# Moving more of the product with C from VectorE to GpSimd in a Mamba scan, from the second image on

## The chip, the cores and the metric

The kernel runs on one core of one Trainium2 chip. The metric is the device time of one execution in microseconds (us). Engines are called PE (TensorE, with PEld for its weight loads), DVE (VectorE), ACT (ScalarE), POOL (GpSimd) and SP (SyncE).

## The reference

Four layers act on x of shape 4 x 384 x 48 x 48; each adds its result to its input. Layer 0, a Mamba block, holds the change. Per image, its 48 x 48 pixels are a sequence of L = 2304 steps, with 768 inner channels and 16 states per channel:

```
dt = softplus(dt @ dt_proj_w.T + dt_proj_b);  A = -exp(A_log)
dA    = exp(dt_t[..., None] * A)
dBx   = dt_t[..., None] * B_t[:, None, :] * x_t[..., None]
h_new = dA * h_prev + dBx
y_t   = einsum('bds,bs->bd', h_new, C_t)
```

The rest of layer 0 is projections, a short convolution, gates, an output projection and a norm. Layer 1 is a 1x1 product, an 8x8 patch transform, a depthwise 3x3 convolution (nine taps) with a gelu gate, and a 1x1 product. Layer 2 is a depthwise 11x11 convolution. Layer 3 mixes four experts with two matrix products each.

## The kernel before

All data is float32. An image's 2304 steps are cut into five chunks of 460 to 464 steps (`CHUNKS`, `NC = 5`). In a chunk the 768 channels are six tiles of 128 partitions, taken as three pairs; a pair of tiles has 2 x 16 states, so a chunk has `LEN = 96` (tile, state) units and the kernel 20 x 96 = 1920. A unit is called u here, and one pass of the main loop is a slot. `where(u)` (L797) gives the chunk i, the pair p, the tile m, the state s and whether the unit is "slow". Within a pair, the position q runs from 0 to 31: an even q and the odd q after it are the two tiles of one state, and they share one row of B and one of C, broadcast to 128 partitions by a DMA from SP (`spread`, L802).

One unit passes through these steps:

- `decay` (L820, ACT): da = exp(dt * A), into one of two PSUM buffers.
- `drive` (L831, POOL): bu = u * B, into one of three SBUF buffers.
- `scan` (L844, DVE): the recurrence along 460 steps from da and bu. In a slow unit it is written to the SBUF buffer g, in any other unit back into da.
- `keep` (L858, ACT): the last column is copied to `carry`, for the next chunk of the same image; the last chunk of an image needs none.
- the product with C: `product_now` (L864, DVE, g = da * C) in a unit that isn't slow, `product` (L873, POOL, g = g * C in place) in a slow one.[...]
- `turned` (L770, PE): g is transposed in four pieces and added up over the states in the PSUM tile y. There are six buffers of g.

The order in each engine's queue is written out by hand in the main loop (L1067 to L1103). Slot u holds, in this order: the ACT steps of the other work, `scan(u)` (in a slow unit followed at once by its `keep`), the other engines' steps of the other work, `product_now(u)` with its `keep`, `decay(u + 2)`, `product(u - 1)` and `drive(u + 3)`. The transposes follow five slots after a slow unit and three slots after another.

The other work is generators of steps (`Task`, `Lane`). The lane `aux` holds the rest of layer 0, with due times by slot. Lane `one` holds layers 1, 2 and the router of the image before (`later`), lane `two` its experts. A `Meter` limits the PE work that the lanes put into a slot to about 2.3 us, by written-in weights. The first image runs with nothing but `aux`; lanes `one` and `two` are filled from the 42nd slot of the second image on. When the 1920 units are over, what is left of the lanes, the last image's layers 1 to 3 and its experts run in a tail, with no scans.

The depthwise taps of layer 1 (L1264 and L1266, DVE) go three to a slot when `slow_slot()` (L1116) is true, else two: a slow slot has no product on DVE. `place[0]` there is the slot that is being written.

Of the kernel before, what the change touches and what calls it, by code (L numbers as in the profile page):

```python
# [21 lines left out]
DI, DS, DTR, DCONV = 768, 16, 24, 4  # L22
# [117 lines left out]
def tile_layers(ctx: ExitStack, tc: tile.TileContext, a: dict, out: bass.AP):  # L140
# [272 lines left out]
    with ExitStack() as first:  # L413
# [123 lines left out]
        NC = len(CHUNKS)  # L537
# [18 lines left out]
        def scans(wk, mm, ring, meter, place, lanes, begin):  # L556
# [240 lines left out]
            def where(u):  # L797
                i, q = divmod(u, LEN)
                p, q = divmod(q, PAIR)
                return i, p, 2 * p + q % 2, q // 2, q % 3 == 0  # L800

            def spread(k, which):  # L802

                if not 0 <= k < N // 2:
                    return
                i, p, m, s, _ = where(2 * k)
                (b, t), c = G[i], st[i]
                n = CHUNKS[t]
                tag = "BC"[which]
                v = wk.tile([P, TM], F32, name=f"{tag}{b}_{t}_{p}_{s}", tag=tag, bufs=3 + which)  # L810
                live[tag, k] = v
                live.pop((tag, k - 3 - which), None)
                nc.sync.dma_start(v[:, :n], c["bc"][which, s, :n].partition_broadcast(P))

            def decay(u):
                i, p, m, s, _ = where(u)
                (b, t), c = G[i], st[i]
                n = CHUNKS[t]
                da = live["da", u] = mm.tile([P, 512], F32, name=f"da{b}_{t}_{m}_{s}", tag="da")
                nc.scalar.activation(  # L820
                    da[:, :n], c["dt", p][:, m % 2, :n], AF.Exp, scale=a_neg[:, m, s : s + 1]
                )

            def drive(u):
                i, p, m, s, _ = where(u)
                (b, t), c = G[i], st[i]
                n = CHUNKS[t]
                bu = live["bu", u] = wk.tile(
                    [P, TM], F32, name=f"bu{b}_{t}_{m}_{s}", tag="bu", bufs=3
                )  # L830
                nc.gpsimd.tensor_mul(  # L831
                    bu[:, :n], c["u", p][:, m % 2, :n], live["B", u // 2][:, :n]
                )
# [280 lines left out]
                ordered[0] = False  # L1114

        def slow_slot():  # L1116
            return place[0] % (2 * DS) % 3 == 0

        def later(b, ring, accr):

# [123 lines left out]
            def finish_strip(hb):  # L1244
# [7 lines left out]
                def taps(ct):  # L1252
                    yield ("dve", 0, (accr, 1))
                    acc, k = sums[ct] = accr.take(f"dw{b}_{hb}_{ct}")
                    v = acc[:, :LB].rearrange("p (h w) -> p h w", w=W)
                    room = 3 if slow_slot() else 2
                    for k in range(9):
                        if not room:
                            yield ("dve",)
                            room = 3 if slow_slot() else 2  # L1260
                        room -= 1
                        src = d["pad", hb][:, ct, k // 3 : k // 3 + 8, k % 3 : k % 3 + W]
                        if k == 0:
                            nc.vector.tensor_scalar_mul(v, src, w_dw[:, ct, 0:1])  # L1264
                        else:
                            nc.vector.scalar_tensor_tensor(  # L1266
                                v, src, w_dw[:, ct, k : k + 1], v, ALU.mult, ALU.add
                            )
# [479 lines left out]
        place = [0]  # L1748
# [187 lines left out]
```

## Time and profile before

| | us |
|---|---|
| median of 3 runs (lowest, highest) | 5467.04 (5466.89, 5471.5) |
| the profiled execution's own time | 5472.59 |
| its span | 5470.3 |
| first to last scan | 88.7 to 4551 |
| first scan of the second image | 1025.0 |

Busy shares of the span: PE 86%, DVE 76%, POOL 57%, ACT 55%. A share is an average over stages that differ: up to 1025 us the first image's scans run alone, from there to 4551 us three images' scans run beside the later layers of the images before, and after that there are no scans. A row of groups gives line, engine, operation, tiles and count, then busy time and mean ns of one, then idle time of the engine before them and what ended it.

### The profile page before, as it was taken

Reading aid. Unit: us, or ns where it says so; the run is one execution under the profiler, and the core shown is the slowest. Engines: PE = TensorE matmul, PEld = TensorE weight load, DVE = VectorE, ACT = ScalarE, POOL = GpSimd, SP = SyncE. Lnnn points to the kernel's source line nnn. Section 1 sums busy time; section 2 is a strip of 40 time slices with the busy share of each in tenths; the row PEclk is TensorE's granted clock in tenths of the full one; section 3 lists DMA queues with packets and bytes.
Section 4 is the critical chain, followed back from the end, with each engine's and each line's share of the span. In section 5 each row is a group of like instructions: output and inputs, shape, how many; then the busy total and the mean of one; then the engine's idle time right before and its main releaser. Section 6 shows DMA issues by size and latency. Waiting matters only on the chain. (4 is left out here: it accounts for less than half of the span.)

```text
span 5470.3 us, 82006 instructions
## 1 busy us (share of the span) xinstructions
PE 4689.8 (86%) x27796; PEld 3688.4 (67%) x27796; DVE 4176.4 (76%) x5806; ACT 2999.9 (55%) x6632; POOL 3124.6 (57%) x2795
## 2 busy tenths in 40 slices
PE   5677677777678989988899999988899999999899
PEld 3445445454447767665678887665678878888799
DVE  5889989999898898899988788899988774443200
ACT  3555555565458765655467655665566753334321
POOL 3878878865567777665567667665666662000000
PEclk8788888798789999999899999999999999999899
DMA  4445445454345555544566566554556564543200
GB/s 121 135 137 147 124 128 146 128 149 124 104 125 148 151 160 163 172 140 140 152 169 174 155 166 175 153 154 130 164 158 169 163 175 145 148 138 102 66 27 23
DMA packets 628393, 758.97 MB, mean 139 GB/s; under 512 B 58869, under 2 KB 622181, under 8 KB 627582
## 3 DMA queue, kind: packets, MB, share of 16 engines
q1 hardware_dynamic: 617668, 751.98, 48.5%
q8 instruction: 221, 3.62, 0.3%
q10 hardware_dynamic: 10298, 1.67, 0.2%
q14 instruction: 206, 1.69, 0.1%
HBM read 663.81 MB, written 89.65 MB: 138 GB/s over the span
## 5 line engine op out<-in xcount | busy, mean ns | idle before, releaser
L831 POOL TENSOR_TENSOR bu<-u,B 128x460 f32<-128x460 f32 (+1 forms) x1920 | 2226.4, 1168 | 1118.2 <-DVE g L844 506.7
L820 ACT ACTIVATE da<-dt,a_neg 128x460 f32<-128x460 f32 (+1 forms) x1920 | 1243.7, 649 | 317.3 <-DVE g L864 223.0
L770 PE MATMUL y<-ident,g 128*115 128x128 f32 (+1 forms) x7680 | 1169.0, 295 | 273.4 <-DVE g L864 202.0
L770 PEld LDWEIGHTS y<-ident,g 128*115 128x115 f32 (+1 forms) x7680 | 1024.1, 185 | 546.9 <-DVE g L864 246.8
L844 DVE TENSOR_TENSOR_SCAN da<-da,carry,bu 128x460 f32<-128x460 f32 (+1 forms) x1008 | 1182.5, 1173 | 69.9 <-ACT da L820 48.7
L873 POOL TENSOR_TENSOR g<-g,C 128x460 f32<-128x460 f32 (+1 forms) x660 | 767.7, 1163 | 197.9 <-ACT carry L858 195.9
L864 DVE TENSOR_TENSOR g<-da,C 128x460 f32<-128x460 f32 (+1 forms) x1260 | 796.4, 632 | 87.1 <-DMA C<-bcd 28.1
L844 DVE TENSOR_TENSOR_SCAN g<-da,carry,bu 128x460 f32<-128x460 f32 (+1 forms) x528 | 616.8, 1168 | 105.6 <-ACT da L820 61.1
L858 ACT COPY carry<-da 128x1 f32<-128x1 f32 x1008 | 159.0, 158 | 948.1 <-DVE g L864 944.8
L1601 PE MATMUL pout<-hr,we 128*128 128x144 f32 x3456 | 488.9, 298 | 49.7 <-ACT hr L1617 30.5
L1601 PEld LDWEIGHTS pout<-hr,we 128*128 128x128 f32 x3456 | 461.1, 199 | 70.2 <-ACT hr L1617 40.6
L1601 PE MATMUL ph<-xe,we 128*128 128x144 f32 x3456 | 471.1, 292 | 15.2 <-DMA xe<-x3d 10.1
L1601 PEld LDWEIGHTS ph<-xe,we 128*128 128x128 f32 x3456 | 448.6, 195 | 30.4 <-DMA xe<-x3d 8.9
L1408 PE MATMUL pc<-band,row 128*128 128x162 f32 (+14 forms) x3456 | 456.2, 285 | 7.1 <-ACT row L1395 7.1
L1408 PEld LDWEIGHTS pc<-band,row 128*128 128x128 f32 x3456 | 443.5, 195 | 11.0 <-ACT row L1395 8.3
L642 PE MATMUL pin<-xch,w_inx 128*128 128x463 f32 (+2 forms) x720 | 332.5, 602 | 33.4 <-DMA xch<-in_x 20.0
L1266 DVE SCALAR_TENSOR_TENSOR dw<-pad,w_dw,dw 128x384 f32<-128x384 f32 x576 | 347.6, 614 | 17.4 <-ACT pad L1241 6.5
L915 PE MATMUL po<-w_out,zs 128*115 128x384 f32 (+1 forms) x960 | 342.4, 497 | 9.3 <-DVE dt L750 7.8
L674 PE MATMUL pinz<-xch,w_inz 128*128 128x460 f32 (+1 forms) x720 | 326.3, 592 | 0.3 <-DVE ye L1633 0.3
L1617 ACT ACTIVATE hr<-ph,nb 128x144 f32<-128x144 f32 x576 | 176.2, 376 | 268.2 <-PE ph L1601 267.8
L844 DVE TENSOR_TENSOR_SCAN da<-da,nil,bu 128x460 f32<-128x460 f32 x252 | 294.8, 1170 | 12.8 <-ACT carry L858 8.5
L1375 ACT ACTIVATE rep<-x,br,wr 128x192 f32<-128x192 f32 x576 | 274.1, 540 | 21.0 <-DVE br L1345 20.9
(202 smaller groups left out, 5725.4 us busy)
## 6 DMA issues: line engine op xcount, KB each, us to landing
B<-bcd SPq DMA_DIRECT2D x768, 230.0 KB, 3.5
C<-bcd SPq DMA_DIRECT2D x768, 230.0 KB, 3.8
B<-bcd SPq DMA_DIRECT2D x192, 232.0 KB, 3.7
C<-bcd SPq DMA_DIRECT2D x192, 232.0 KB, 4.0
xe<-x3d SPq DMA_DIRECT2D x192, 216.0 KB, 2.9
ye<-y3d SPq DMA_DIRECT2D x144, 216.0 KB, 2.8
y3d<-ye SPq DMA_DIRECT2D x96, 216.0 KB, 2.2
xs<-x1d SPq DMA_DIRECT2D x24, 576.0 KB, 4.9
```

The costliest lines, as they stand in the source:

```text
L642: nc.tensor.matmul(ps[:, lo : halo + n], lhsT=w_inx[:, k, bass.ts(j, P)], rhs=c["x"][:, k, lo : halo + n], start=k == 0, stop=k == CT - 1,)
L674: nc.tensor.matmul(ps[:, :n], lhsT=w_inz[:, k, bass.ts(j, P)], rhs=c["x"][:, k, DCONV - 1 : DCONV - 1 + n], start=k == 0, stop=k == CT - 1,)
L770: nc.tensor.matmul(c["y", m][:w, bass.ts(k, P)], lhsT=src[:, bass.ts(k, w)], rhs=ident, is_transpose=True, start=c["terms", m] == 1 and k ...
L820: nc.scalar.activation(da[:, :n], c["dt", p][:, m % 2, :n], AF.Exp, scale=a_neg[:, m, s : s + 1])
L831: nc.gpsimd.tensor_mul(bu[:, :n], c["u", p][:, m % 2, :n], live["B", u // 2][:, :n])
L844: nc.vector.tensor_tensor_scan(here[:, :n], da[:, :n], bu[:, :n], last if t else nil[:, 0:1], ALU.mult, ALU.add,)
L864: nc.vector.tensor_mul(live["g", u][:, :n], live["h", u][:, :n], live["C", u // 2][:, :n])
L873: nc.gpsimd.tensor_mul(g[:, :n], g[:, :n], live["C", u // 2][:, :n])
L915: nc.tensor.matmul(ps[:w, :C], lhsT=c["zs"][:, m, bass.ts(k, w)], rhs=w_out0[:, m, :], start=m == 0, stop=m == MT - 1,)
L1266: nc.vector.scalar_tensor_tensor(v, src, w_dw[:, ct, k : k + 1], v, ALU.mult, ALU.add)
L1408: nc.tensor.matmul(d["acc2"][0][:, : BANDS[k] * W].rearrange("p (h w) -> p h w", w=W)[:, lo - edges[k] : hi - edges[k], xlo:xhi], lhsT=d[" ...
L1601: nc.tensor.matmul(ps[:, bass.ts(m, EB)], lhsT=w[:, k, bass.ts(m, P)], rhs=of[:, k, :], start=k == 0, stop=k == CT - 1,)
```

## The change

Before, a unit is slow when q mod 3 is 0: 11 of the 32 units of a pair of tiles. After, this holds in the first image (i < 5) only; from the second image on a unit is slow when q mod 4 is 0 or 1, which are the two tiles of every other state: 16 of 32. `slow_slot` takes the second rule for all slots.

```diff
@@ -797,7 +797,8 @@
             def where(u):
                 i, q = divmod(u, LEN)
                 p, q = divmod(q, PAIR)
-                return i, p, 2 * p + q % 2, q // 2, q % 3 == 0
+                slow = q % 3 == 0 if i < NC else q % 4 < 2
+                return i, p, 2 * p + q % 2, q // 2, slow
...
         def slow_slot():
-            return place[0] % (2 * DS) % 3 == 0
+            return place[0] % 4 < 2
```

## The prediction, made before the result was known

> **What bounds the kernel now.** I first read the groups of the page for the four operations of a unit.
>
> ```profile
> L831 POOL TENSOR_TENSOR bu<-u,B 128x460 f32<-128x460 f32 (+1 forms) x1920 | 2226.4, 1168 | 1118.2 <-DVE g L844 506.7
> ...
> L844 DVE TENSOR_TENSOR_SCAN da<-da,carry,bu 128x460 f32<-128x460 f32 (+1 forms) x1008 | 1182.5, 1173 | 69.9 <-ACT da L820 48.7
> L873 POOL TENSOR_TENSOR g<-g,C 128x460 f32<-128x460 f32 (+1 forms) x660 | 767.7, 1163 | 197.9 <-ACT carry L858 195.9
> L864 DVE TENSOR_TENSOR g<-da,C 128x460 f32<-128x460 f32 (+1 forms) x1260 | 796.4, 632 | 87.1 <-DMA C<-bcd 28.1
> ```
>
> The same product costs 632 ns on DVE and 1163 ns on POOL. POOL's drives sit idle for 1118 us, most of it until a DVE scan gives a bu buffer back: POOL follows DVE.
>
> Next I cut the time at each chunk's first scan and read the busy times of the stretches. The columns are stretch, length, and busy us (count) of PE, PEld, DVE, ACT, POOL, then the granted PE clock and DMA. The first row is the first image, the second the three images that the change touches, the third the tail; then come some of the 15 chunks.
>
> ```profile
> 89.00:1025.00 936.00, 669.39 (x2960) 455.95 (x2960) 846.93 (x1035) 536.55 (x1122) 771.98 (x686) 0.80 0.48 135
> 1025.00:4551.00 3526.00, 3107.01 (x18334) 2403.62 (x18335) 3067.40 (x4193) 2152.39 (x4742) 2344.11 (x2087) 0.93 0.54 154
> 4551.00:5470.00 919.00, 866.46 (x6354) 798.64 (x6353) 233.84 (x516) 287.90 (x736) 4.96 (x15) 0.96 0.31 88
> ```
>
> ```profile
> 1025.00:1230.00 205.00, 159.71 (x738) 106.24 (x738) 188.06 (x251) 126.44 (x277) 157.78 (x144) 0.90 0.53 146
> 1230.00:1505.00 275.00, 197.89 (x762) 122.15 (x762) 248.81 (x355) 136.48 (x295) 156.46 (x142) 0.78 0.40 114
> ...
> 2656.00:2906.00 250.00, 222.27 (x1350) 178.09 (x1349) 213.41 (x296) 152.09 (x353) 156.62 (x138) 0.92 0.57 161
> 2906.00:3143.00 237.00, 230.26 (x1603) 198.98 (x1602) 186.64 (x243) 168.64 (x397) 154.70 (x138) 0.98 0.57 162
> ...
> 3591.00:3855.00 264.00, 221.30 (x1141) 160.04 (x1140) 250.66 (x362) 150.51 (x336) 156.28 (x141) 0.93 0.48 139
> ```
>
> The reader sees two bounds that alternate. In the first image DVE is busy 90% and PE 72%. In the other three both are at 87 to 88%, but not at the same time: the chunks at 1025, 1230, 1505, 2380 and 3591 us have DVE at 90 to 95% and PE at 72 to 84% (**DVE's chunks**); those at 1733, 2906, 3143, 3362, 4097 and 4336 us have PE at 93 to 97% (**PE's chunks**); those at 1948, 2148, 2656 and 3855 us have both at 85 to 92% (**shared**). POOL is busy 66% there.
>
> Last, the waits of POOL and then those of DVE from 1025 to 4551 us, in us, times and longest:
>
> ```profile
> POOL bu L831 <- DVE g L844: 425.8, 363, 8.5
> POOL bu L831 <- DVE da L844: 417.8, 374, 4.8
> POOL g L873 <- ACT carry L858: 165.0, 142, 3.6
> ```
>
> ```profile
> DVE da L844 <- POOL bu L831: 1.3, 1, 1.3
> ...
> DVE g L844 <- POOL bu L831: 0.8, 2, 0.6
> ```
>
> DVE waits for POOL for 2 us in 3526. PE waits for POOL's g there 22 times, 11 us.
>
> **What the Trainium skill says.** "GPSIMD Engine Reference", section 3.1, puts a two-input elementwise operation on GpSimd at 1.96 times VectorE's time; here it is 1163 / 632 = 1.84, so the trace agrees roughly. "SBUF — State Buffer", section "Who interferes with whom", says that a DVE instruction with at most one SBUF input, outside the two-port modes, doesn't contend with GpSimd. Scan and product on DVE read da from PSUM and one tensor from SBUF, and POOL's product stays between 1144 and 1200 ns while DVE is busy 87% of the time: the trace agrees, so I give the added POOL work no contention. "Perfetto Trace Analysis", section "GPSIMD Engine Instruction", advises spacing of starts over reported spans: starts of back-to-back POOL products lie 1.12 to 1.13 us apart (52.28 to 53.41 after 1000 us), and I use 1.13.
>
> **The change, part by part.** *Removed from DVE.* A chunk has 3 x 11 = 33 slow units now and 3 x 16 = 48 after, so 15 products leave DVE in each of 15 chunks, 225 in all. Busy time: 225 x 0.632 = 142 us. The next DVE instruction starts some 0.55 us after a product's start (1057.44 to 1057.99), so the queue gets shorter by 225 x 0.56 = 126 us, 8.4 us per chunk. What of it counts depends on the chunk. DVE's five chunks: all, 5 x 8.4 = 42 us. The four shared ones: half, 17 us, since PE would bind next. PE's six: a tenth, 5 us; there DVE already waits for PE. Sum: 64 us.
>
> *Added to POOL.* 225 x 1.163 = 262 us busy, 17 us per chunk, against 44 to 119 us of POOL's idle time in each chunk. POOL goes from 2344 to 2606 us, or 75% of some 3470 us. The first image shows what this does: POOL is busy 82% there, and yet DVE waits for POOL 6 us (8.2 in the whole run less 2.1), and PE for POOL's g 30 us over 165 slow products, 0.18 each; later it is 11 us over 496, 0.02 each. For 75% I take 0.06 for each of the 225 moved: 14 us lost. Bounds: nothing, and 0.18 x 225 = 41 us.
>
> *The order in POOL's queue.* In four slots POOL now gets four drives and two products, 6 x 1.13 = 6.8 us, 1.70 per slot; chunks run at 2.1 to 2.9. Two products come in slots running, each ahead of a drive that the scan three slots later waits for. Three bu buffers cover this: after scan 1, POOL runs drive 4, product 1 and drive 5 by 3.4 us, and scan 5 begins 1.1 x 3 + 0.55 x 2 = 4.4 us after the end of scan 1 even with nothing else on DVE. No DMA is moved: B and C rows come as before from SP, and both tiles of a state read C while it is held.
>
> *Waits that go.* A slow unit's da is free when its scan ends and not after the taps and the product behind it. ACT's decay two units on waits less (164 us in 118 waits on L864 in these images). DVE waited 109 us for da there; a quarter of the L864 units go, but ACT's own work ends part of it, so I take nothing, at most 20 us. ACT's carry copies get a little dearer (187 ns from g, 158 from da): 180 x 0.03 = 5 us on an engine 61% busy, hidden by its idle time.
>
> *Taps.* Nine taps at three or two a slot fill four slots under either rule, wherever they start, so the lanes advance as before. In four slots of taps DVE is relieved by its products only. In the tail the slot counter stands still: followed to its end, the loop stops at 1960. By the old rule that isn't slow (1960 mod 32 is 8), by the new it is (1960 mod 4 is 0): the last image's taps go three at a time instead of two. DVE is busy 234 of 919 us there and PE 866, so I take 0, within 10 us either way.
>
> Total: 64 - 14 = 50 us. The profiled execution took 5472.6 us (span 5470.3 and 2.3 around it), 5.6 over the median of 5467.0. Against its own time that gives 5422.6; against the median, **5417 us**.
>
> **Rivals.** *PE takes it all.* PE is at 88% over the three images; where DVE gets ahead, PE's queue fills the room. For it: six chunks at 93 to 97%, and a tail that runs on PE alone. Against it: PE stands at 72 to 84% in the five DVE chunks. It leaves a few us in those, say 1.5 each: 8 us, 5459.
>
> *All of it counts.* If DVE's order held back PE in the shared and PE chunks as well (y's transposes wait 174 us on PEld and PE for L864 there), the 126 us come off less some 11 for POOL: 5352. Against: PE at 0.97.
>
> *Slower: POOL becomes the pacer.* A product waits for the ACT carry copy, which stands behind other ACT work, and the next drive waits behind the product. Now 142 of 496 wait, 1.16 us each. If every product waited 1.3 us, four slots would take 6.8 + 2.6 = 9.4 us, 226 us per chunk. The chunks at 1025, 1733, 1948, 3143 and 4336 us would then grow by 21, 11, 26, 7 and 11 us, 76 in all; the others save 64 - 15 = 49, and PE's waits for g cost the 14 of above: 76 - 49 + 14 = 41 us slower, 5508. It decides from a wait of about 1.2 us for every product. Against it: a POOL that is behind finds the copy made, so this wait shrinks as POOL fills.
>
> **How the numbers follow.** About 0.2%, 11 us, is what a measurement of this kernel can tell from no change. The partial gain (5380 to 5450) has 0.58, the whole gain 0.08, PE taking it 0.17 (0.06 of it still faster by more than 11 us), POOL as pacer 0.17. So faster 0.58 + 0.08 + 0.06 = 0.72, same 0.11, slower 0.17. The range is 5365 to 5480: it leaves out the whole gain and most of the pacer case.
>
> **What would show it.** After, L864 should count 1035 and L873 885. The chunks of the five should lose 7 to 9 us each with DVE's share unchanged, the PE chunks 0 to 3. DVE's waits on bu should stay below 15 us and PE's on POOL's g below 60. The first image should be within 2 us of 936. I am wrong if POOL's bu ends DVE waits of over 40 us, if PE chunks shrink as much as DVE's, or if the tail moves by more than 10 us.

## The result, and the profile after

The changed kernel takes 5433.7 us (median of 4 runs, 5427.7 to 5441.4) against 5468.3 for the kernel before on the same chip. The ratio is 0.994, with an interval of 0.9928 to 0.9951: 35 us faster. The forecast was 50 us and 5417. The profiled execution has a span of 5434.5 us, 35.8 less than before.

I cut it at first scans as before. The stretches of the changed kernel (columns as in the prediction):

```profile
87.00:1026.00 939.00, 672.94 (x2962) 459.04 (x2963) 847.78 (x1036) 536.64 (x1123) 773.34 (x686) 0.80 0.46 135
1026.00:4535.00 3509.00, 3099.08 (x18346) 2403.84 (x18345) 2947.77 (x3968) 2138.88 (x4744) 2584.41 (x2312) 0.92 0.53 154
4535.00:5434.00 899.00, 857.50 (x6343) 792.69 (x6340) 233.06 (x515) 287.14 (x736) 4.34 (x15) 0.97 0.31 90
```

With the exact starts of the scans, the span's 35.8 us split up as follows. "Scans" are the three images that the change touches.

| us | before | after | difference | forecast |
|---|---|---|---|---|
| until the first scan | 88.7 | 86.9 | -1.8 | 0 |
| first image | 936.4 | 938.7 | +2.3 | 0, within 2 |
| scans of images 2 to 4 | 3526.5 | 3509.2 | -17.3 | -50 |
| tail | 918.8 | 899.8 | -19.0 | 0, within 10 |

One profile per kernel stands behind such a table. In the kernels below that leave the first image as it is, it took between 930 and 940 us, so a difference under some 5 to 10 us in one stage is not to be read alone. The profiled execution can also lie off its kernel's median: 5.6 us above it in the kernel before, 2.8 above it in the changed one.

That the total came near the forecast is in part luck. The stage in which the products were moved gave a third of what it was to give, and the tail, in which no product was moved, gave more than the scans did.

The groups of the four operations after (lines from L800 on have moved by one or two):

```profile
L832 POOL TENSOR_TENSOR bu<-u,B 128x460 f32<-128x460 f32 (+1 forms) x1920 | 2227.1, 1169 | 813.1 <-DVE g L845 432.4
...
L874 POOL TENSOR_TENSOR g<-g,C 128x460 f32<-128x460 f32 (+1 forms) x885 | 1029.5, 1163 | 252.1 <-ACT carry L859 245.3
...
L865 DVE TENSOR_TENSOR g<-da,C 128x460 f32<-128x460 f32 (+1 forms) x1035 | 654.3, 632 | 93.5 <-PE y L770 32.9
```

The counts are those of the prediction, 1035 and 885, and the durations are unchanged (632 and 1163 ns): nothing got dearer by contention. DVE's busy time in the three images fell by 120 us (3067 to 2948; neighbours that overlap count once in it, so this is to be held against the 126 us of queue in the prediction, not against the 142), but its idle time rose from 459 to 561 us. The question is what filled the 102 us. The waits of DVE there (us, times, longest), first in the kernel before:

```profile
DVE g L844 <- ACT da L820: 61.9, 20, 8.2
DVE da L844 <- ACT da L820: 47.1, 58, 3.2
...
DVE g L844 <- PE y L770: 6.4, 6, 1.7
...
DVE g L864 <- PE y L770: 2.0, 3, 1.3
```

and in the changed kernel:

```profile
DVE da L845 <- ACT da L821: 101.7, 76, 8.1
...
DVE g L845 <- ACT da L821: 40.3, 44, 3.5
...
DVE g L865 <- PE y L770: 32.9, 30, 3.8
...
DVE g L845 <- POOL bu L832: 26.0, 28, 3.5
...
DVE g L845 <- PE y L770: 9.9, 12, 1.6
...
DVE da L845 <- POOL bu L832: 5.5, 5, 2.4
```

Three of them grew (both kinds of scan and the product together): the wait for ACT's da from 109 to 142 us, the wait for PE to give a g back (y L770) from 8 to 43 us, and the wait for POOL's bu from 2 to 32 us. No single wait took the place of the products.

Some chunks of the changed kernel, in the same columns; they answer to those that the prediction shows:

```profile
1026.00:1232.00 206.00, 160.94 (x742) 106.11 (x740) 181.24 (x235) 125.05 (x277) 172.28 (x159) 0.89 0.48 142
1232.00:1496.00 264.00, 192.75 (x762) 119.87 (x762) 239.91 (x341) 134.94 (x295) 173.26 (x157) 0.79 0.40 120
...
2643.00:2893.00 250.00, 216.78 (x1338) 174.60 (x1339) 205.49 (x280) 149.09 (x348) 171.97 (x153) 0.92 0.56 160
2893.00:3134.00 241.00, 232.19 (x1607) 200.51 (x1605) 179.76 (x229) 170.27 (x402) 172.65 (x154) 0.97 0.56 161
...
3582.00:3847.00 265.00, 224.64 (x1162) 163.42 (x1162) 242.76 (x347) 150.05 (x335) 173.49 (x156) 0.92 0.48 138
```

Only the second of these lost what was forecast: 275 to 264 us, with DVE's share still at 91% (240 of 264). In the chunks at 1026 and 3582 us the length stayed, and DVE's share fell from 92 to 88% and from 95 to 92%: the room was made and not used.

### The profile page after: what moved, and what is told of

It is laid out like the page before. It is cut to its first block, busy times and chain, and to the rows that moved or that the text cites. A ratio compares the mean times of both kernels' runs of the same rounds, so it can differ in the third digit from the quotient of the medians.

```text
span 5434.5 us, 81808 instructions
## 1 busy us (share of the span) xinstructions
PE 4677.1 (86%) x27796; PEld 3685.9 (68%) x27796; DVE 4056.7 (75%) x5581; ACT 2985.7 (55%) x6632; POOL 3365.5 (62%) x3020
## 5 line engine op out<-in xcount | busy, mean ns | idle before, releaser
L770 PE MATMUL y<-ident,g 128*115 128x128 f32 (+1 forms) x7680 | 1144.9, 298 | 266.2 <-DVE g L865 162.6
L770 PEld LDWEIGHTS y<-ident,g 128*115 128x115 f32 (+1 forms) x7680 | 1016.4, 188 | 493.2 <-DVE g L865 198.0
L874 POOL TENSOR_TENSOR g<-g,C 128x460 f32<-128x460 f32 (+1 forms) x885 | 1029.5, 1163 | 252.1 <-ACT carry L859 245.3
L845 DVE TENSOR_TENSOR_SCAN da<-da,carry,bu 128x460 f32<-128x460 f32 (+1 forms) x828 | 971.7, 1174 | 121.7 <-ACT da L821 94.1
L845 DVE TENSOR_TENSOR_SCAN g<-da,carry,bu 128x460 f32<-128x460 f32 (+1 forms) x708 | 820.0, 1167 | 104.8 <-ACT da L821 40.2
L865 DVE TENSOR_TENSOR g<-da,C 128x460 f32<-128x460 f32 (+1 forms) x1035 | 654.3, 632 | 93.5 <-PE y L770 32.9
L859 ACT COPY carry<-da 128x1 f32<-128x1 f32 x828 | 130.6, 158 | 832.0 <-DVE g L865 828.6
L661 DVE SCALAR_TENSOR_TENSOR xc<-pin,conv_w,xc 128x460 f32<-128x460 f32 (+1 forms) x360 | 249.3, 692 | 33.9 <-ACT xc L655 20.3
```

Of the source, the lines that this page charges most:

```text
L770: nc.tensor.matmul(c["y", m][:w, bass.ts(k, P)], lhsT=src[:, bass.ts(k, w)], rhs=ident, is_transpose=True, start=c["terms", m] == 1 and k ...
L845: nc.vector.tensor_tensor_scan(here[:, :n], da[:, :n], bu[:, :n], last if t else nil[:, 0:1], ALU.mult, ALU.add,)
L865: nc.vector.tensor_mul(live["g", u][:, :n], live["h", u][:, :n], live["C", u // 2][:, :n])
L874: nc.gpsimd.tensor_mul(g[:, :n], g[:, :n], live["C", u // 2][:, :n])
```

## The experiments

### Which half of the change gave what

The kernels of this part were timed in three groups, each on one chip, and the median of the kernel before on these chips lay between 5463 and 5472 us. Each ratio is against the kernel before on the same chip, so between groups the ratios compare better than the times. None of these kernels differs from the kernel before by as much as 2%.

The change has two lines, and they act in different stages. The first kernel keeps only the new rule in `where`:

```diff
         def slow_slot():
-            return place[0] % 4 < 2
+            return place[0] % (2 * DS) % 3 == 0
```

> The new rule for the products alone; slow_slot keeps the old rule, so the taps of the tail go two at a time as in the kernel before. Theory A (the gain has two sources: the scans lost 17 us, the tail 19 us, the latter through slow_slot alone): about 17 us under the kernel before, some 5450; tail 915 to 922 us from last scan to end. Rival B (the tail got shorter because the lanes came out of the scans in another state, not because of slow_slot): the whole gain stays, 5433, tail near 900.

Measured: 5446.8 us, ratio 0.9964 (0.9951 to 0.9978). The tail took 918.7 us, as before the change, and the scans 3507.0, as after it. The second kernel is the kernel before with the new rule in the tail's slots alone:

```diff
         def slow_slot():
-            return place[0] % (2 * DS) % 3 == 0
+            return place[0] % 4 < 2 if place[0] >= 1920 else place[0] % (2 * DS) % 3 == 0
```

> The kernel before with one edit: slow_slot is true once the slot counter is past the last unit, so the tail's taps go three at a time; products and taps beside the scans as before. Theory A: 15 to 22 us under the kernel before, some 5449, tail near 900, scans within 3 us of before. Rival B: within 5 us of the kernel before.

Measured: 5456.0 us, ratio 0.9977 (0.9968 to 0.9987); scans 3525.1, tail 904.4. The two savings, 0.36% and 0.23%, add up to the 0.6% of the whole change. Without the new `slow_slot` the tail gains nothing, and with it alone it gains 14 of the 19 us. So the tail's gain comes from `slow_slot`.

What it does there is seen at layer 1's taps and at the outputs of layer 2 (`xb`), whose first and last start stand after the durations. The last scan ends at 4551 us in the kernel before and in the second experiment, and at 4535 us in the changed kernel. First the kernel before:

```profile
L1266 DVE SCALAR_TENSOR_TENSOR dw<-pad,w_dw,dw x144: 604/615/624, 4686.8 to 4973.6; 128x384 f32<-128x384 f32 x144
```

```profile
L1429 DVE TENSOR_TENSOR xb<-pc,xb x15: 607/656/658, 5005.8 to 5124.0; 128x480 f32<-128x480 f32 x9, 128x432 f32<-128x432 f32 x6
```

Then the changed kernel:

```profile
L1267 DVE SCALAR_TENSOR_TENSOR dw<-pad,w_dw,dw x144: 604/615/624, 4667.1 to 4898.1; 128x384 f32<-128x384 f32 x144
```

```profile
L1430 DVE TENSOR_TENSOR xb<-pc,xb x15: 606/657/659, 4972.0 to 5088.8; 128x480 f32<-128x480 f32 x9, 128x432 f32<-128x432 f32 x6
```

These 144 taps take 287 us before and 231 us after. DVE is busy for 145 of the 287 us, so it has room; the taps are given to it two or three at a step of the lane, and fewer steps pass sooner. With the last scan's end as zero, the taps end at 423 us before and at 363 after, 60 us sooner, and the last `xb` starts at 573 and at 554, 19 us sooner. From there to the end of the span it is 346 us in both kernels (5470.3 - 5124.0 and 5434.5 - 5088.8). The other 41 of the 60 us are not won: the third image's experts, whose last outputs are at 4973 us before and at 4962 after, share PE with layer 1 and, counted from the last scan, end no sooner.

Where the 19 us come from is seen between layer 1's end and the first `xb`, where layer 2 begins with a norm, a chain of small steps on several engines. First the kernel before, then the changed one up to the end of the experts and from there on:

```profile
4974.00:5006.00 32.00, 24.29 (x112) 17.25 (x113) 6.61 (x20) 12.76 (x30) 0.55 (x1) 0.63 0.22 65
```

```profile
4898.00:4962.00 64.00, 60.84 (x449) 55.09 (x448) 13.30 (x31) 13.79 (x42) 0.55 (x1) 1.00 0.48 136
4962.00:4972.00 10.00, 10.00 (x88) 10.00 (x87) 0.61 (x2) 8.74 (x21) 0.00 (x0) 1.00 0.14 42
```

Before, the taps and the experts end together, and layer 1's last products and the beginning of layer 2 stand alone: PE is busy for 24 of 32 us, at a granted clock of 0.63. After, the taps end 64 us before the experts, whose products fill PE meanwhile, and the clock is 1.00. From the last scan to the last `xb` PE was idle for 26 us before and for 16 after, and its busy time fell from 547 to 538 us.

In the last experiment below all nine taps go in one step, and its tail takes 899.7 us: past three taps nothing more comes.

### Is it POOL's added work that holds the scans back?

This kernel is the changed one without the products that POOL got in addition. Five slow units in each pair of tiles keep their scan into g but get no product with C at all (so the time is that of a POOL with its old load, in the new order).

```diff
                 i, p, m, s, slow = where(u)
-                if slow:
+                left = i >= NC and u % PAIR in (1, 5, 13, 17, 25)
+                if slow and not left:
```

> The changed kernel, but from the second image on 15 of the 48 products of POOL in a chunk are left out (those at positions 1, 5, 13, 17 and 25 of a pair: g goes to the transposes without its factor C). DVE is relieved as in the change, POOL has as many products as before. Theory P (what the added products cost on POOL's way, in waits of PE and DVE for it, ate the missing 33 us of the scans' gain): scans 25 us or more shorter than in the changed kernel, some 5405. Rival E (PE and the rest would take the time anyway): scans within 8 us of the changed kernel, 5426 to 5436.

Measured: 5427.4 us (0.9926, 0.9912 to 0.994). The scans took 3499.9 us, 9 less than after:

```profile
1022.00:4522.00 3500.00, 3097.08 (x18339) 2401.01 (x18340) 2945.80 (x3968) 2138.95 (x4742) 2338.99 (x2088) 0.93 0.54 155
```

POOL's busy time is back at 2339 us, DVE has its 2946 us, and DVE's idle time is 554 us, still almost 100 above the kernel before. So POOL's additional work costs some 9 us (6 by the medians, about the scatter of a stage); 8 of them stand in the first of the 15 chunks. Its amount isn't what swallowed the gain. The test says less of the order in POOL's queue: at positions 8 and 9, 20 and 21, 28 and 29 of a pair two of its products are still neighbours, and DVE still waits 22 us for bu and PE 55 us for POOL's g.

### The same number of products in another order

Every other unit is slow here, not two of every four. The count per pair is 16 in both.

```diff
-                slow = q % 3 == 0 if i < NC else q % 4 < 2
+                slow = q % 3 == 0 if i < NC else q % 2 == 0
...
         def slow_slot():
-            return place[0] % 4 < 2
+            return place[0] % 2 == 0
```

> The changed kernel with the same half of the units slow, but every other unit (q even) instead of two and two; slow_slot follows. POOL's load per four slots is the same and more even; a slow scan then needs the g buffer of the slow unit six before it, whose transposes stand only one slot earlier. Theory P with bunching (two POOL products in a row delay a drive and the second product): 10 to 20 us faster than the changed kernel. Rival G (the six g buffers tie DVE to PE): as much slower, since every slow scan waits at its start. Neither: within 6 us of 5433.

Measured: 5396.9 us, ratio 0.9874 (0.9859 to 0.9889): 73 us faster than before, more than twice the gain of the change, and more than any of the expectations gave it. Its scans:

```profile
1026.00:4488.00 3462.00, 3088.00 (x18341) 2400.52 (x18342) 2949.41 (x3968) 2133.15 (x4742) 2584.56 (x2312) 0.93 0.55 156
```

All busy times are those of the changed kernel within 11 us, POOL's too (2585 and 2584), and the stretch is 47 us shorter. Against the kernel before the scans are 65 us shorter: 49 in DVE's five chunks, 10 in the four shared ones and 5 in PE's six. That is nearly the 64 us (42, 17 and 5) that the prediction gave the removed products before it took anything off. **The order in which the slow units stand is worth some 40 us in the scans, 47 by these two profiles.**

The 47 and the 65 are upper values: this profile is of the fastest of its four executions, 5 us under their median, and the medians put the two orders 37 us apart. Two more alternating kernels below have scans of 3463.5 and 3465.6 us, and two more kernels in the order of the change 3507.0 and 3504.5. The new rule also moves the taps beside the scans; for the two-and-two order the first experiment shows that this is worth some 2 us (3507.0 and 3509.2).

Its `slow_slot` also gives three taps at 1960, and its tail, 902.0 us, is that of the changed kernel within 3.

What the order alters on PE: a slow unit's transposes follow five slots later and another's three slots later. With two slow units and two others, units 0 and 2 fall on slot 5, units 1 and 3 on slot 6, and slots 7 and 8 get none. With alternation every slot gets one unit's. The timeline of PE around 2.46 ms shows it (start, duration, tiles, number of matmuls run together). The changed kernel:

```profile
2460.37 1.13 PE L770 MATMUL y<-ident,g 128*115 128x128 f32 x8
...
2463.66 1.03 PE L770 MATMUL y<-ident,g 128*115 128x128 f32 x8
...
2471.53 1.04 PE L770 MATMUL y<-ident,g 128*115 128x128 f32 x8
```

and the alternating kernel:

```profile
2454.44 0.60 PE L770 MATMUL y<-ident,g 128*115 128x128 f32 x4
...
2457.19 0.60 PE L770 MATMUL y<-ident,g 128*115 128x128 f32 x4
```

x8 is two units in a row, and after two such bunches no unit comes for almost 7 us (2464.69 to 2471.53); x4 is one unit. Over the three images the alternating kernel has 871 runs of x4 and 198 of x8, one of them at 2458.30; the changed kernel has none of x4, 554 of x8 and 61 of x16. Four explanations were open: these bunches on PE, the rings of g and bu that are too short for the new order, the rhythm of long and short slots itself, and POOL's queue, in which two products now follow in slots running. The first two were tested.

The same alternation in the first image too (against the alternating kernel):

```diff
-                slow = q % 3 == 0 if i < NC else q % 2 == 0
+                slow = q % 2 == 0
```

> The alternating order in the first image too, where POOL is busy 82% already: 240 products of POOL in its 480 units instead of 165. POOL would have 480 x 1.13 + 240 x 1.13 = 814 us and more to do in 936 us. If POOL then sets the pace there, the first image gets 10 to 40 us longer; if DVE's relief counts, it gets up to 20 us shorter. The three other images as in the alternating order, within 5 us.

Measured: 5395.7 us (0.9871, 0.9856 to 0.9887), first image 941.5 us against 938.4: no gain there that can be measured, though 75 more products left DVE in it. POOL was busy 90% of that image (849 of 941 us).

### The rings

To make room for one more g or bu, `dx` was written over `xc`, which isn't needed after it, in all three kernels of this group; the first of them has only that and is the control for the other two.

```diff
-                    dx = wk.tile([P, TM], F32, name=f"dx{b}_{t}_{m}", tag="dx", bufs=1)
+                    dx = c["xc"][:, m]
                     nc.scalar.activation(
-                        dx[:, :n], c["xc"][:, m, :n], AF.Copy, scale=d_col[:, m : m + 1]
+                        dx[:, :n], dx[:, :n], AF.Copy, scale=d_col[:, m : m + 1]
                     )
```

> The changed kernel with dx (the skip term D * x, one SBUF buffer of its own) written in place over xc, which nothing reads any more by then. It frees room for one more buffer and is the control for the next two. It also takes away the wait for that one buffer: PE waits some 33 us for dx in the changed kernel's scans, so 0 to 10 us faster than 5433; theories R (below) and S (below) both expect no more than that.

Measured: 5432.0 us (0.9944, 0.993 to 0.9959), scans 3504.5: as the changed kernel.

Seven g buffers (`tag="g", bufs=7`, where there were 6):

> The control with seven buffers of g instead of six. Theory R (the ring of g ties DVE's products to PE's transposes of the slot before, and two and two makes both kinds collide): DVE's wait for PE before g, 45 us, falls below 15 and the scans get 25 us or more shorter than in the control, most of the way to the 3462 us of the alternating order. Rival S (the rhythm of two short and two long slots doesn't fit any of the rings that reach two or three slots ahead, da, bu and g alike): the wait falls, but turns into others, and the scans get less than 12 us shorter.

Measured: 5428.5 us (0.9933, 0.9917 to 0.9948), scans 3498.2, 6 less than the control and within its scatter. DVE's wait for PE to give g back fell from 43 us in the changed kernel, 36 in the control, to 1. The other waits took its place:

```profile
DVE da L845 <- ACT da L821: 112.9, 83, 8.2
...
DVE g L845 <- ACT da L821: 56.1, 53, 5.0
```

The two rows were 101.7 and 40.3 in the changed kernel. The wait was removed, and most of it turned into one for da: the ring of g by itself is not the bound.

Four bu buffers (`tag="bu", bufs=4`, where there were 3):

> The control with four buffers of bu instead of three, so that a drive on POOL waits for the scan one earlier. Theory P (POOL's two products in slots running delay the drives): DVE's wait for bu, 31 us in the scans, disappears and the scans get 20 us or more shorter than in the control. Rivals R and S: less than 10 us.

Measured: 5432.3 us (0.9937, 0.9922 to 0.9952), as the control by the medians. The scans of the profile, 3515.7 us, are 11 above the control's, but it is of an execution 7 us above its median. DVE's waits for bu were still 26 us (34 in the control), so the ring's length isn't what makes them; POOL itself being late isn't excluded by this.

### PE's bunches

From the second image on, the transposes of the units that aren't slow follow four slots later instead of three (and the copy of y for the odd tile one slot later), so that slots 5, 6, 7 and 8 get one, two, one and none.

```diff
-                    for h, e in ((1, u - 4), (0, u - 5)):
+                    for h, e in ((1, u - (4 if u - 4 < LEN * NC else 5)), (0, u - 5)):
...
                         add(u - 5, True)
-                        add(u - 3, False)
+                        for lag in (3, 4):
+                            if (u - lag < LEN * NC) == (lag == 3):
+                                add(u - lag, False)
```

> The changed kernel, but from the second image on the transposes of the units that DVE multiplies stand four slots after the unit instead of three (and the copy of y for the odd tile one slot later). In the changed kernel two slots of four have two units' transposes each and two have none; here it is 1, 2, 1, 0. The ring of g is no looser. Theory B (PE's transposes in bunches are what costs): scans 20 us or more shorter than the 3509 us of the changed kernel. Rivals R, S and P: within 10 us of it.

Measured: 5416.8 us (0.9916, 0.9901 to 0.9931), scans 3490.7, 18 less than in the changed kernel and 14 less than in the control of the rings, which ran on the same chip and whose median is 15 us higher. So the place of the transposes is a part of it. PE's wait for DVE's product fell from 42 to 17 us, while that for POOL's rose. In the changed kernel:

```profile
PE y L770 <- DVE g L865: 42.0, 25, 4.0
...
PE y L770 <- POOL g L874: 27.0, 14, 4.7
```

and with the shift:

```profile
PE y L770 <- POOL g L874: 42.9, 21, 4.7
...
PE y L770 <- DVE g L865: 16.7, 12, 3.2
```

The opposite test puts the same shift into the alternating kernel. There it makes bunches: two units in every odd slot, none in the even ones.

> The alternating order with the transposes of DVE's units one slot later, so that every odd slot has two units' transposes and every even one none; before it was one per slot. Theory B (bunches of transposes are part of what two and two cost, some 18 of 47 us): scans 12 to 25 us longer than the 3462 us of the alternating order. Rival S (only the rhythm of the scans and products on DVE counts, and the later transposes helped two and two for another reason, such as less waiting of PE for g): within 6 us.

Measured: 5471.0 us (1.0, 0.999 to 1.0009), 74 more than with alternation alone. The profile is of the fastest of 14 executions, 11 us under their median, and its scans, 3527.3 us, are 66 longer. One row of DVE's waits grew the most; with alternation alone it was

```profile
DVE g L845 <- PE y L770: 26.7, 25, 3.3
```

and with the shift

```profile
DVE g L845 <- PE y L770: 167.6, 122, 6.0
```

A slow scan writes into the g that unit u - 6 had, and that unit's transposes, in slot u - 1, now stand together with those of u - 5. The shift cost far more than the 12 to 25 us expected. The bunch alone doesn't explain it: in PE's queue the transposes of u - 6 still come first of the two, and four more matmuls take half a microsecond. Where the long wait comes from was not followed further. PE's own wait for DVE's product, with the weight loads, fell from 158 to 21 us here; it fell in the two-and-two order too, which got faster, so this wait doesn't decide.

Then the changed order with both remedies, the shift and seven g (with dx in place):

> The changed kernel, still two and two, with dx in place, seven buffers of g and the transposes of DVE's units one slot later. If bunches and the ring of g are separate parts, their gains add: scans near 3482 us, 27 below the changed kernel. If they are the whole of what the order costs, 3462 as in the alternating order. Theory S (the rest is the rhythm of two short and two long slots): 3478 to 3490, with DVE's wait for ACT's da in the first fast slot still near 50 us.

Measured: 5415.3 us (0.9899, 0.9885 to 0.9913), scans 3490.7, the same as the shift alone. By the ratios it is 9 us faster than the shift alone, but the intervals overlap: no gain of the ring on top of the shift is shown. Some 20 to 29 us to the alternating order remain (5395.7 us for an alternating kernel on the same chip, and scans of 3461.7).

The two orders differ in the waits for POOL. These are the waits of PE's transposes (with their weight loads) for POOL's g and of DVE's scans for POOL's bu, as the views of lines L770 and L845 give them (us, times), first in the changed order with both remedies, then with alternation:

```profile
  POOL g L874: 99.0, 60
...
  POOL bu L832: 28.3, 32
```

```profile
  POOL g L874: 31.5, 45
...
  POOL bu L832: 5.7, 13
```

No kernel moved POOL's products within its queue, so what these waits cost isn't shown.

Last, alternation with seven g (and dx in place) and nine taps a step in the tail. This line stands in two places:

```diff
-                    room = 3 if slow_slot() else 2
+                    room = 9 if place[0] >= 1960 else 3 if slow_slot() else 2
```

> A version meant to beat both: the alternating order with dx in place and seven buffers of g, and in the tail nine taps at a step instead of three. Theory R for this order (a slow scan waits for g, 32 us): 5 to 15 us off the scans' 3462. Tail: 0 to 15 us under 902. Together 5375 to 5392.

Measured: 5390.7 us (0.9855, 0.984 to 0.9869), the lowest time of all kernels here. Its interval overlaps that of alternation alone, and its scans (3465.6) missed the expected 3447 to 3457, so the two extras can't be said to bring anything. What beats both kernels is the alternation, by about 73 us on the kernel before and 37 on the changed one.

## Why the prediction was right and wrong

**Direction and size: nearly right, with luck: two errors partly cancel.** The scans gave 33 us less than forecast and the tail 19 more.

**The removed products, 64 us: about right as what they can be worth, not as what this order yields.** The alternating kernel moves as many and gains 65 in the scans by its profile (56 by the medians, less the tail's 17), in nearly the split that was forecast. In the changed kernel DVE's five chunks lost 19 us (forecast 42; one of them 11, two nothing), the shared ones 11 (17), and PE's grew by 13 (forecast -5), 10 of it in the first of them.

**The order, priced at nothing: this is the step that failed.** The working counted whether POOL could deliver its drives in time, and three bu buffers do cover that nearly: DVE's waits for bu were 32 us, twice the bound of 15 and below the 40 at which the prediction was to be wrong, and a fourth buffer gave nothing. But it looked at POOL's queue alone. The same order also sets the slots in which PE transposes, and the rhythm in which DVE asks for da and g. The order costs some 40 us, 47 by the profiles. Of these the shift on PE recovers 14 to 18. What the rest is stays open. One candidate is POOL: its additional products cost some 9 us in the two-and-two order, and what they cost in the alternating one wasn't measured, but there PE and DVE wait for POOL far less (the rows above). Another is the rhythm of the slots. The mean length of a slot by its place in four is 2.18, 2.17, 2.85, 2.55 us after and 2.06, 2.67, 2.29, 2.60 with alternation. With two buffers of da, ACT runs at most two units ahead, so a pair of short slots would find da not ready; DVE's wait for da, still the largest in the changed order with both remedies (140 us), fits that, but the alternating kernel waits for da almost as long (137 us). So both are only argued: neither more da buffers nor POOL's products in other slots were tried.

**POOL late with g, -14 us: about right in size.** Leaving the added products out gives 9 (6 by the medians), against bounds of 0 and 41. PE's waits for POOL's g (66 us, 45 times) were a little over the bound of 60.

**Contention, carry copies, freed da: as forecast.** POOL's product stayed between 1143 and 1202 ns with POOL 84% busy in the chunk at 1026 us, which agrees once more with the Trainium skill's "SBUF — State Buffer", section "Who interferes with whom", by which a VectorE instruction with at most one input from SBUF doesn't contend with GpSimd outside the two-port modes (the scan also reads one column of `carry`). The copies took 191 ns from g and 159 from da in the median, as before; no run shows their 5 us by themselves. The earlier-free da brought nothing that can be seen: DVE's wait for it grew.

**Taps in the scans: right.** DVE's other work in each chunk is the same in number before and after and within 2 us in time; the taps moved only within their four slots.

**The tail, 0 within 10: wrong.** The prediction had followed the counter to 1960 and seen that the taps would go three at a time, and then priced this by DVE's busy share (234 of 919 us). DVE's work doesn't limit the tail, but the steps in which layer 1 hands it over set when layer 1 ends, and so whether the beginning of layer 2 falls under the experts' products on PE or stands alone. 19 us came from there (14 when done alone).

**Rivals.** PE takes it all: no, the alternating order's scans are 65 us shorter at the same work on PE. POOL as the pacer: no; POOL was busy 86% in the densest chunk (173 of 200 us from 1945 us on), and taking its additional load away brought 9 us, not the 90 between that rival and the forecast.

## What to carry to other kernels

When work is moved from one engine to another at a given ratio, count, slot by slot, what each engine's queue gets over one period, and not only the engine that takes the work; here an even placing was the better of the two tried. Before a step is priced at nothing because its engine is idle, ask what hands it its work and what can start when it ends; in the tail here the step size counted and the engine's load did not. A rule that also paces another stage (here `slow_slot` in the tail) is a second change, to be tested by itself.

## What was unexpected on the hardware

One slot's shift of small matmuls moved the alternating kernel from 5397 to 5471 us (ratios 0.987 and 1.000) and the two-and-two kernel from 5434 to 5417 (0.994 and 0.992), with the same work on every engine. In this kernel, with queues in a written order and rings of two, three and six buffers, the spacing of the work mattered as much as its amount: the 225 products that left DVE, 120 us of its busy time, were worth 17 us in the scans in one order and 65 us in the other, by these profiles.
